# Gated cross-attention with a mixture of experts: where the routing's small sums, factors and statistics are computed

## The chip, the cores and the metric

The kernel runs on one core of a Trainium2 chip. The core has five engines with instruction lists of their own: PE multiplies matrices, DVE does vector work, ACT applies functions, POOL does small vector work and issues indirect DMAs (gathers and scatters), and SP issues plain DMAs. Each engine takes its list in order; an instruction that waits holds up all behind it on that engine. The metric is device time in microseconds for one execution, the median of the runs. Less is better.

## The reference, cut to what matters

There are four batches of 512 tokens with 256 features. First comes cross-attention in which a token looks at four neighbouring rows of a context, then a feed-forward layer with eight experts, of which each token uses two:

```python
x = x + tanh(g_xattn[0]) * xattn(layernorm(x), ctx_1024, itok, Wq, Wkv, Wo)   # rows itok, itok-1, itok-2, itok-3
h = layernorm(x)
probs = softmax(h @ gate_w.T)                 # 8 experts
top_v, top_i = top_k(probs, 2)
out = 0
for e in range(8):
    y = silu(h @ w1[e] + b1[e]) @ w2[e] + b2[e]     # 256 -> 1024 -> 256
    out += y * (weight of e if e is in top_i, else 0)
x = x + tanh(g_ffn[0]) * out
```

All is in float32.

## The kernel before, in words

The 2048 tokens are 16 tiles of 128, four to a batch. The kernel has two overlapping parts.

**Attention, a tile at a time.** `rows_of` gathers a tile's four context rows from a DRAM table of projected keys and values (POOL, L240; three buffers, two tiles ahead; the first gather needs the table of batch 0, stored at L228). `stage_ask` makes the queries (PE, `pq`, L426). `stage_attend` multiplies and sums (DVE, `prod`, `sc`, L439 to L485; the exponential `ex` on ACT, L459) and leaves `ao` (or `v`, for the first tiles). `stage_out` turns it (`pa`, L497/L499), copies it (`aoT`, ACT L512), multiplies by the output weights (`po`, L515), and DVE adds the residual (`x_sb`, L518), the gate's logits (`lg`, L526) and the statistics of the second norm (L257, L258). The first norm's statistics, which give `rsa`, the factor inside `ex`, are made for a whole batch by `normalise_first`: four pairs of BATCH_NORM instructions on DVE and two instructions on POOL (L266, L268).

**Routing.** Tiles form groups of 2, 2, 1, 1, 1, 1, 2, 2, 2, 2. When a group's last tile is out, `stage_route` finds the two best experts per token (`best`, `which`), the exponentials of the logits (`exg`, L592), their sum `gs`, the one-hot choices `pick`, and `pos`, the row of the scratch table `xs` to which each token's copy goes. Each expert owns a region of `xs`. `pos` needs a running count of tokens per expert: `run` (DVE, L565) over earlier tiles, multiplied by a matrix of ones on PE (L571), plus a triangular product within the tile (L568), plus the region's first row `ebase` (L595). POOL computes `rs`, the norm's factor (L266, L268), ACT writes the normalised `rows` (L609), and POOL scatters them (L377), two scatters per tile. In order not to hold up tile 4, the code lets its `rs` go ahead of half of the scatters of the group before it (L582).

`queue` runs after groups from tile 4 on (after tiles 5, 6, 7, 8, 10, 12, 14 and 16, counted as tiles finished). From the counts (`pn`, L666) it names the next full blocks of 128 rows, each with an expert and a first row: 3, 2, 2, 2, 4, 4, 4, 4 of them, and all that is left at the end. At its end it updates `took`, `take`, `issued` and `nextrow` (L727 to L733).

**Blocks.** There are 37 blocks in this run's main path. SP loads a block's weights (`w1s`, L752) and its rows (`xg`, L770, which waits for the scatters so far). PE turns the rows (`pxg`, L783), DVE copies them (`xgT`, L786), PE multiplies up (`ph`, L798), ACT applies Silu (`hT`, L810), PE multiplies down (`py`, L825), DVE weighs (`yw`, L836), and POOL adds the result to the output (L839).

What orders the work: `in_order` chains DVE's attention and routing instructions in the order in which they are written. The order on the other engines, and where the blocks' instructions come between, is fixed when the program is built. So PE's list mixes pieces of attention with pieces of blocks, and the mix can't adapt at run time.

On SP, the first loads are `xT_sb` and `x_sb` of batch 0 (L137, L140), then the store of the first table (L228), then `x_sb` of batch 1 (L322).

Of the kernel before, what the change touches and what calls it, by code (L numbers as in the profile page):

```python
# [9 lines left out]
F32 = mybir.dt.float32  # L10
# [6 lines left out]
P = 128  # L17
# [6 lines left out]
def gated_xattn_moe(  # L24
# [117 lines left out]
    first_loads = [load_xT(0), load_x(0)]  # L142
# [142 lines left out]
    with tc.tile_pool(  # L285
        name="ps_t", bufs=1, space=bass.MemoryType.PSUM
    ) as ps_t:
        with in_order(PE, mybir.EngineType.DVE):
# [7 lines left out]
            stored = project_near(kv_first, ps_t, src0, 0)  # L296
# [25 lines left out]
    behind(load_x(1), stored)  # L322
# [29 lines left out]
    def _layers(ctx, is_near):  # L352
# [16 lines left out]
        run = keep.tile([P, NT + 1, E], F32, name="run")  # L369
        nc.vector.memset(run[:, 0, :], 0.0)  # L370
# [159 lines left out]
        def stage_route(g):  # L530
# [15 lines left out]
            for j in range(GT):  # L546
# [4 lines left out]
            nc.vector.tensor_tensor(  # L551
                ex, lg, best[:, :, 0:1].to_broadcast([P, GT, E]), ALU.subtract
            )
# [9 lines left out]
            for j in range(GT):  # L563
                t = t0 + j
                nc.vector.tensor_add(run[:, t + 1, :], run[:, t, :], pick[:, j, :])  # L565
# [5 lines left out]
            nc.tensor.matmul(  # L571
                pp,
                all_one,
                run[:, tiles, :].rearrange("p t e -> p (t e)"),
                start=False,
                stop=True,
            )
# [12 lines left out]
            behind(named, root)  # L590
            for j in range(GT):
                nc.scalar.activation(ex[:, j, :], ex[:, j, :], AF.Exp, scale=rs[:, j : j + 1])  # L592
            yield
            place = gate.tile([P, GMAX, E], F32, tag="place", name=f"place_{g}")[:, 0:GT]
            nc.vector.tensor_tensor(  # L595
                place,
                pp.rearrange("p (t e) -> p t e", e=E),
                ebase.unsqueeze(1).to_broadcast([P, GT, E]),
                ALU.add,
            )  # L600
            nc.vector.tensor_tensor(
                hot, hot, place.unsqueeze(2).to_broadcast([P, GT, TOPK, E]), ALU.mult
# [4 lines left out]
            nc.vector.scalar_tensor_tensor(nm, mv[:, :, 0], -1.0, rs, ALU.mult, ALU.mult)  # L607
# [10 lines left out]
            gs = gate.tile([P, GMAX], F32, tag="gs", name=f"gs_{g}")[:, 0:GT]  # L618
            nc.vector.tensor_reduce(gs, ex, AX.X, ALU.add)
            nc.vector.reciprocal(gs, gs)  # L620
            yield
# [19 lines left out]
        issued = keep.tile([P, E], F32, name="issued")  # L641
        nc.gpsimd.memset(issued, 0.0)
# [14 lines left out]
        took = keep.tile([P, E + 1], F32, name="took")  # L657
        nc.gpsimd.memset(took, 0.0)

        def queue(tiles, w, last=False):  # L660


            q = len(ready)
# [367 lines left out]
```

## Time and profile before

| | us |
|---|---|
| median of 3 runs | 399.97 (399.18 to 400.34) |
| the profiled execution | 399.22 |
| its span, first to last instruction | 397.5 |
| PE busy | 343.4 |
| DVE busy | 195.7 |
| ACT busy | 160.1 |
| POOL busy | 131.3 |
| first product of the first block (`ph`, L798) | starts at 85.2 |

A float32 product is two records of PE (MATMUL) and two weight loads (PEld) in the profile: what is called a pair below. In lines of the timeline the columns are the start and the busy time in us, the engine, the line, the operation, the tiles written and read, the shapes, the number of instructions merged and, in brackets, how long the engine had been idle and what released it.

### The profile page before, as it was taken

Reading aid. Unit: us, or ns where it says so; the run is one execution under the profiler, and the core shown is the slowest. Engines: PE = TensorE matmul, PEld = TensorE weight load, DVE = VectorE, ACT = ScalarE, POOL = GpSimd, SP = SyncE. Lnnn points to the kernel's source line nnn. Section 1 sums busy time; section 2 is a strip of 40 time slices with the busy share of each in tenths; the row PEclk is TensorE's granted clock in tenths of the full one; section 3 lists DMA queues with packets and bytes.
Section 4 is the critical chain, followed back from the end, with each engine's and each line's share of the span. In section 5 each row is a group of like instructions: output and inputs, shape, how many; then the busy total and the mean of one; then the engine's idle time right before and its main releaser. Section 6 shows DMA issues by size and latency. Waiting matters only on the chain. (4 is left out here: it accounts for less than half of the span.)

```text
span 397.5 us, 7304 instructions
## 1 busy us (share of the span) xinstructions
PE 343.4 (86%) x2153; PEld 306.9 (77%) x2153; DVE 195.7 (49%) x663; ACT 160.1 (40%) x445; POOL 131.3 (33%) x164
## 2 busy tenths in 40 slices
PE   4877646089999989999999999999999999999960
PEld 1545534078998989898889989999999999999950
DVE  2288797879789989798947301101111111111000
ACT  1121202027756666767576334234243342342410
POOL 4421444513365354453724322112112122121311
PEclk9869696579999999999999999999999999999995
DMA  7899999589969988987667897776767767755111
GB/s 259 269 399 423 419 425 378 177 287 313 299 187 343 237 274 280 336 238 233 205 158 189 281 222 234 236 196 164 246 176 211 214 171 235 195 167 143 18 28 17
DMA packets 43577, 94.22 MB, mean 237 GB/s; under 512 B 14844, under 2 KB 31996, under 8 KB 35720
## 3 DMA queue, kind: packets, MB, share of 16 engines
q1 hardware_dynamic: 33506, 66.23, 51.2%
q0 software_dynamic: 9168, 26.09, 23.0%
q10 hardware_dynamic: 854, 1.33, 1.0%
q8 instruction: 21, 0.34, 0.3%
q14 instruction: 28, 0.23, 0.2%
HBM read 79.90 MB, written 13.73 MB: 236 GB/s over the span
## 5 line engine op out<-in xcount | busy, mean ns | idle before, releaser
L798 PE MATMUL ph<-xgT,w1s 128*128 128x128 f32 x1184 | 143.0, 276 | 0.0
L798 PEld LDWEIGHTS ph<-xgT,w1s 128*128 128x128 f32 x1184 | 140.3, 192 | 2.3
L825 PE MATMUL py<-w_sb,hT 128*128 x592 | 135.7, 380 | 1.4 <-DVE yw L836 0.7
L810 ACT ACTIVATE hT<-ph,b1s 128x128 f32<-128x128 f32 x296 | 83.6, 372 | 113.6 <-issue 95.7
L825 PEld LDWEIGHTS py<-w_sb,hT 128*128 128x128 f32 x592 | 109.2, 190 | 15.7 <-issue 2.1
L839 POOL DMA_INDIRECT out<-yw,ms x37 | 58.7, 1586 | 158.3 <-issue 69.5
L836 DVE SCALAR_TENSOR_TENSOR yw<-py,ms,b2s 128x256 f32<-128x256 f32 x37 | 17.8, 482 | 76.3 <-PE py L825 72.4
L786 DVE COPY xgT<-pxg 128x256 f32<-128x256 f32 x37 | 15.6, 421 | 69.5 <-PE pxg L783 69.4
L377 POOL DMA_INDIRECT xs<-rows,pos x32 | 35.0, 1094 | 30.6 <-ACT rows L609 7.3
L240 POOL DMA_INDIRECT g<-near,idx_near x16 | 17.6, 1098 | 37.4 <-DVE v L472 23.3
L439 DVE TENSOR_TENSOR prod<-pq,g 128x1024 f32<-128x1024 f32 x16 | 19.4, 1213 | 5.9 <-DMA g<-near,idx_near 5.9
L426 PE MATMUL pq<-wqg_sb,xT_sb 128*128 128x264 f32 x64 | 20.5, 449 | 1.5 <-DVE prod L439 1.1
L515 PE MATMUL po<-wo_sb,aoT 128*128 128x264 f32 x64 | 19.8, 436 | 2.0 <-ACT aoT L512 1.4
L472 DVE TENSOR_TENSOR v<-g,pr 128x1024 f32<-128x1024 f32 x16 | 19.6, 1224 | 0.5
L810 ACT ACT_TABLE_LOAD x13 | 16.7, 1283 | 7.7 <-issue 5.2
L442 DVE TENSOR_REDUCE sc<-prod 128x64 f32<-128x1024 f32 x16 | 19.5, 1217 | 0.4
L868 ACT ACTIVATE b2s<-b2s,ms 128x256 f32<-128x256 f32 x37 | 19.5, 532 | 0.0
L426 PEld LDWEIGHTS pq<-wqg_sb,xT_sb 128*128 128x128 f32 x64 | 14.0, 225 | 5.2 <-DVE prod L439 2.2
L497 PE MATMUL pa<-ident,ao 128*128 128x128 f32 x24 | 5.6, 308 | 13.2 <-DVE ao L485 13.1
L515 PEld LDWEIGHTS po<-wo_sb,aoT 128*128 128x128 f32 x64 | 12.1, 207 | 5.6 <-ACT aoT L512 4.0
L783 PE MATMUL pxg<-ident,xg 128*128 128x128 f32 x74 | 14.5, 278 | 1.5 <-DMA xg<-xs 1.5
L497 PEld LDWEIGHTS pa<-ident,ao 128*128 128x128 f32 x24 | 3.3, 165 | 14.5 <-issue 11.6
(128 smaller groups left out, 262.6 us busy)
## 6 DMA issues: line engine op xcount, KB each, us to landing
w1s<-in_w SPq DMA_DIRECT2D x37, 1024.0 KB, 5.4
w_sb<-in_w SPq DMA_DIRECT2D x8, 1024.0 KB
b2s<-in_b SPq DMA_DIRECT2D x37, 128.0 KB, 5.2
xg<-xs SPq DMA_DIRECT2D x37, 128.0 KB, 5.5
xT_sb<-in_xT SPq DMA_DIRECT2D x4, 512.0 KB, 11.3
x_sb<-in_x SPq DMA_DIRECT2D x4, 512.0 KB
out<-x_sb SPq DMA_DIRECT2D x6, 256.0 KB
xs<-padrow SPq DMA_DIRECT2D x9, 136.0 KB, 3.7
```

Source lines behind the costliest of these rows:

```text
L377: i = nc.gpsimd.indirect_dma_start(out=xs, out_offset=bass.IndirectOffsetOnAxis(ap=where, axis=0), in_=rows, in_offset=None,).ins
L426: nc.tensor.matmul(pq, xT_sb[:, t, k, :], wqg_sb[:, k, :], start=(k == 0), stop=(k == KD - 1))
L439: seen[t] = nc.vector.tensor_tensor(prod, pq[:, 0:D].unsqueeze(1).to_broadcast([P, KW, D]), gt[:, :, 0:D], ALU.mult).ins
L442: nc.vector.tensor_reduce(sc.rearrange("p o h -> p (o h)"), prod.rearrange("p o (h d) -> p (o h) d", d=HD), AX.X, ALU.add,)
L472: nc.vector.tensor_tensor(v.rearrange("p o (h d) -> p o h d", d=HD), gt[:, :, D : 2 * D].rearrange("p o (h d) -> p o h d", d=HD), pr.unsqu ...
L515: nc.tensor.matmul(po, aoT[:, k, :], wo_sb[:, k, :], start=(k == 0), stop=(k == KD - 1))
L798: m = nc.tensor.matmul(ph[:, i, :], w1s[:, k, ts(f, P)], xgT[:, k, :], start=(k == 0), stop=(k == KD - 1),).ins
L810: hidden = nc.scalar.activation(hT[:, f, :], ph[:, i, :], AF.Silu, bias=b1s[:, f : f + 1]).ins
L825: m = nc.tensor.matmul(py, hT[:, f, :], w2_sb[:, bass.ds(be_v * NF + f, 1), :].rearrange("p o d -> p (o d)"), start=(f == 0), stop=(f == N ...
L836: outs[s] = nc.vector.scalar_tensor_tensor(yw, py, ms[:, 0:1], b2s, ALU.mult, ALU.add).ins
L839: acc = nc.gpsimd.indirect_dma_start(out=out, out_offset=bass.IndirectOffsetOnAxis(ap=ms[:, 1:2].bitcast(I32), axis=0), in_=yw, in_offset= ...
L868: behind(nc.scalar.activation(b2s, b2s, AF.Copy, scale=ms[:, 0:1]).ins, hidden)
```

## The change

There are five edits.

1. `x_sb` of batch 1 is loaded right after that of batch 0, before the store of the first table, and `normalise_first(1)` is called right after `normalise_first(0)`, ahead of the first tile's attention, not after it.
2. `run` starts from the regions' first rows (in one partition only, since the ones-matrix sums over partitions), so the addition of `ebase` (`place`, L595) goes. `run` has one entry for a group, not for a tile, and its additions move from DVE to POOL. The product of ones with `run` now takes the count before the group; within a group the second tile adds a product with the first one's `pick`, and `queue` adds one product for each tile of the group.
3. ACT's exponential takes the logits themselves, with `-best * rs` as its bias, and gives the sum `gs` through its accumulator output. The subtraction (L551) and the sum (L619) go from DVE. The factors `less` (`-rs`, `-best * rs`) and `nm` are computed on POOL, three instructions for a group.
4. `issued` is gone: `queue` subtracts `nextrow`. `took`, `take` and `nextrow` are computed on POOL.
5. The reciprocal of `gs` is taken after `pos` as before, but now waits for ACT directly.

```diff
-    first_loads = [load_xT(0), load_x(0)]
+    first_loads = [load_xT(0), load_x(0), load_x(1)]
...
-    behind(load_x(1), stored)
...
-        run = keep.tile([P, NT + 1, E], F32, name="run")
-        nc.vector.memset(run[:, 0, :], 0.0)
+        run = keep.tile([P, len(GROUPS) + 1, E], F32, name="run")
+        nc.gpsimd.memset(run[:, 0, :], 0.0)
+        nc.gpsimd.tensor_copy(run[0:1, 0, :], ebase[0:1])
+        picks = {}
...
-            nc.vector.tensor_tensor(
-                ex, lg, best[:, :, 0:1].to_broadcast([P, GT, E]), ALU.subtract
-            )
+            gs = gate.tile([P, GMAX], F32, tag="gs", name=f"gs_{g}")[:, 0:GT]
...
-            for j in range(GT):
-                t = t0 + j
-                nc.vector.tensor_add(run[:, t + 1, :], run[:, t, :], pick[:, j, :])
+            picks[g] = pick
...
-            nc.tensor.matmul(
-                pp,
-                all_one,
-                run[:, tiles, :].rearrange("p t e -> p (t e)"),
-                start=False,
-                stop=True,
-            )
+            for j in range(GT):
+                for k in range(j):
+                    nc.tensor.matmul(
+                        pp[:, j * E : (j + 1) * E], all_one, pick[:, k, :], start=False, stop=False
+                    )
+                nc.tensor.matmul(
+                    pp[:, j * E : (j + 1) * E],
+                    all_one,
+                    run[:, g, :],
+                    start=False,
+                    stop=(j == GT - 1),
+                )
...
+            less = stat.tile([P, 3, GMAX], F32, tag="less", name=f"less_{g}")[:, :, 0:GT]
+            nc.gpsimd.tensor_scalar(less[:, 0], rs, -1.0, None, ALU.mult)
+            nc.gpsimd.tensor_tensor(nm, mv[:, :, 0], less[:, 0], ALU.mult)
+            nc.gpsimd.tensor_tensor(less[:, 1], best[:, :, 0], less[:, 0], ALU.mult)
             for j in range(GT):
-                nc.scalar.activation(ex[:, j, :], ex[:, j, :], AF.Exp, scale=rs[:, j : j + 1])
+                nc.scalar.activation(
+                    ex[:, j, :],
+                    lg[:, j, :],
+                    AF.Exp,
+                    bias=less[:, 1, j : j + 1],
+                    scale=rs[:, j : j + 1],
+                    accum_out=gs[:, j : j + 1],
+                )
+            count = run[:, g, :]
+            for j in range(GT):
+                nc.gpsimd.tensor_add(run[:, g + 1, :], count, pick[:, j, :])
+                count = run[:, g + 1, :]
             yield
-            place = gate.tile([P, GMAX, E], F32, tag="place", name=f"place_{g}")[:, 0:GT]
...
-            nc.vector.scalar_tensor_tensor(nm, mv[:, :, 0], -1.0, rs, ALU.mult, ALU.mult)
...
-            nc.vector.tensor_reduce(gs, ex, AX.X, ALU.add)
+            yield
             nc.vector.reciprocal(gs, gs)
-            yield
...
-            nc.tensor.matmul(pn, all_one, run[:, tiles, :], start=True, stop=True)
+            GT = GROUPS[g][1]
+            nc.tensor.matmul(pn, all_one, run[:, g, :], start=True, stop=False)
+            for j in range(GT):
+                nc.tensor.matmul(pn, all_one, picks[g][:, j, :], start=False, stop=(j == GT - 1))
...
-                nc.vector.tensor_scalar(took[:, 1 : E + 1], ends, float(w), None, ALU.min)
+                nc.gpsimd.tensor_scalar(
+                    took[:, 1 : E + 1], ends, float(w), float(P), ALU.min, ALU.mult
+                )
                 take = gate.tile([P, E], F32, tag="take", name=f"take_{q}")
-                nc.vector.tensor_tensor(take, took[:, 1 : E + 1], took[:, 0:E], ALU.subtract)
-                nc.vector.scalar_tensor_tensor(
-                    issued, take, float(P), issued, ALU.mult, ALU.add
-                )
-                nc.vector.scalar_tensor_tensor(
-                    nextrow, take, float(P), nextrow, ALU.mult, ALU.add
-                )
+                nc.gpsimd.tensor_tensor(take, took[:, 1 : E + 1], took[:, 0:E], ALU.subtract)
+                nc.gpsimd.tensor_add(nextrow, nextrow, take)
...
             normalise_first(0, after=gathers)
+            normalise_first(1, after=gathers)
...
-                if i in (0, RAMP, RAMP + 2):
+                if i in (RAMP, RAMP + 2):
                     normalise_first(1 + (i + 1) // TPB)
```

## The prediction

> **What bounds the kernel now.** I read the page's 40 slices first, then busy time by stretches, then the chain of waits, then the timeline of the stretches where PE is not full. The chain that ended last says nothing here (four pieces at the very end), so the bound is read from the stretches. In the first fence (busy time by stretches; columns: length, busy time and count of PE, PEld, DVE, ACT, POOL, then granted clock, DMA share, GB/s), see that PE does next to nothing from 70 to 80 us while DVE is full, and is full without a break after 240.
>
> ```profile
> 70.00:80.00 10.00, 0.20 (x1) 0.23 (x2) 8.80 (x35) 0.57 (x2) 5.57 (x7) 0.57 0.53 175
> ...
> 100.00:110.00 10.00, 10.00 (x74) 9.54 (x75) 8.07 (x38) 6.92 (x18) 3.70 (x4) 1.00 0.96 298
> ...
> 240.00:280.00 40.00, 40.00 (x272) 37.55 (x271) 4.86 (x11) 14.26 (x48) 7.73 (x5) 1.00 0.73 210
> ```
>
> From 85 us to about 385 us PE is never idle for long: all its waits from 84 to 240 us add up to about 4 us, most of it for `ao`. So the time is (when the first block's `ph` starts, 85 us) + (PE's work behind it) + (about 4 us). The change can act on the first by shortening DVE's path up to 80 us, and on the second by the products that it adds. The next fence, the timeline around the first group of one tile (tile 4), shows the path to the first block: POOL computes `rs`, then issues the last two scatters of the group before, and only then copies `tokid` (L586) and scatters tile 4; DVE meanwhile goes on (L620).
>
> ```profile
> 67.80 0.62 POOL L268 TENSOR_TENSOR rs<-v_b,mhalf 128x1 f32<-128x1 f32 x1
> ...
> 68.61 1.06 POOL L377 DMA_INDIRECT xs<-rows,pos  x1 [0.20 <-issue]
> ...
> 69.69 0.16 DVE L620 RECIPROCAL gs<-gs 128x1 f32<-128x1 f32 x1
> ...
> 69.98 0.96 POOL L377 DMA_INDIRECT xs<-rows,pos  x1 [0.30 <-issue]
> ...
> 70.95 0.20 POOL L586 COPY rows<-tokid 128x8 int32<-128x8 int32 x1
> ```
>
> The third fence, a little later, shows what a small product costs once PE is full: `pp`, `pp`, `pn` and the next `ph` start 0.22 us apart, though only 8 columns move.
>
> ```profile
> 86.45 0.36 PE L568 MATMUL pp<-pick,upto 128*128 128x8 f32 x2
> ...
> 86.67 0.37 PE L571 MATMUL pp<-run,all_one 128*128 128x8 f32 x2
> ...
> 86.89 0.37 PE L666 MATMUL pn<-run,all_one 128*128 128x8 f32 x2
> ...
> 87.11 2.70 PE L798 MATMUL ph<-xgT,w1s 128*128 128x128 f32 x22
> ```
>
> The fourth, for the out stage of tile 0: `po`, then `pq`, then DVE's residual.
>
> ```profile
> 31.49 1.16 PE L515 MATMUL po<-wo_sb,aoT 128*128 128x264 f32 x4 [0.46 <-ACT aoT L512]
> ...
> 32.49 1.05 PE L426 MATMUL pq<-wqg_sb,xT_sb 128*128 128x264 f32 x4
> ...
> 33.70 0.48 DVE L518 SCALAR_TENSOR_TENSOR x_sb<-po,tg,x_sb 128x256 f32<-128x256 f32 x1
> ```
>
> **The change, part by part** (later is plus).
>
> *1. Statistics of batch 2 first.* Their eight DVE instructions stand at 25.75 to 27.88, 2.13 us on DVE's path. They move to 14.1, where DVE waits 5.89 us for the first gather: 2.13 us saved there. But on SP the load of `x_sb` (512 KB) now stands ahead of the table's store, for which the first gather (13.50) waits. Behind it wait the second and third gather on POOL and `prod` on DVE. Bounds for the delay d: none, if the load only fills the idle share of the DMA engines (0.72 to 0.83 busy from 10 to 13 us); 1.9 us, if 0.52 MB go ahead at the 272 GB/s of 11 to 12 us. I take 0.5: both loads and the store had passed by 14 us anyway (share 0.25 from 14 to 15). On POOL the two-instruction chain for batch 2 is split around the third gather; its first half needs the statistics, about 16.3 us, and that gather started at 16.47, so nothing is lost.
>
> What is late next: the built order puts `pq` of tile 3 ahead of `po` of tile 0. `pa` of tile 0 ends at 31.04 (+d; it hangs on `ex` of tile 0, not on the moved statistics), then `pq` about 1.0, then `po` 1.16: L518 starts at 33.25+d, not 33.70. DVE would be ready at 31.57+d, and waits 1.7 us. So of 2.13 us saved only 0.45 survive, less d: **+0.05** (-0.45 to +1.45). The deleted memset (0.07 us, in a wait for a load) counts nothing; POOL's added copy of `ebase` delays only the second gather by 0.2, which is read only at 27.88.
>
> *2. Groups of tiles 0-1 and 2-3.* DVE loses subtraction, two `run` additions, `place`, `nm` and the sum, but its list then waits for `gs`. In the built order POOL adds the first `pick` to `run` **before** `rs`. So in the first group `rs` starts after `pick`, about 42.85 instead of 42.08. Then on POOL come `tokid`, an addition, and three small instructions, priced by L266 and L586 at 0.19 each and 0.15 to 0.27 apart: ends about 44.45. ACT does one `rows` (0.55) and then both exponentials (0.49 for two): the reciprocal starts about 45.5, not 45.24. Meanwhile `pp` has grown from four records to eight, at 0.24 each at the slow clock of that stretch (0.66 mean), and lands at about 44.6 against 44.34: no cover is left for an early finish either. With something for the accumulator and the bias operand, which no row shows (0 to 0.3): +0.35. Second group, same sum: 64.1 instead of 63.54, and on ACT `aoT` of tile 3 now stands behind both `rows` and both exponentials (63.09 becomes 64.6), so `po` (2.13 at the slow clock) ends near 67.1 and L518 (66.28) is +0.85. Together **+1.2** (0.5 to 2).
>
> [...]
>
> *3. Group of tile 4.* The built order on POOL reads: two scatters, first half of `rs`, `rs`, two scatters, `tokid`, `less`, the `run` addition, `nm`, `less` again, two scatters. The code moves only `rs` ahead of the older scatters, so the new factors stand behind them. DVE's reciprocal waits for ACT's exponential, that for `less`, and that for the scatters. By the rows: `rs` ends 68.42, `tokid` starts 2.53 later (70.95), then about 1.0 for the small ones, 0.3 for the exponential (L592), 0.05 to 0.1 per handover: reciprocal 3.75 after `rs`, where it was 1.27 (69.69). **+2.5** (2.0 to 3.0). Queued behind the waiting reciprocal are `left` and all of the first `queue`, hence the first `w1s` load, and the attention of tile 5. `rows` of tile 4 and its two scatters shift by nearly as much, hence `xg`.
>
> *4. Tail of the first `queue`.* L727 to L733, 0.58 us of DVE, go to POOL, which has time there: **-0.5**. `nextrow` is next read one tile later.
>
> So the first `ph` starts about **3.2 us later** (2 to 6), since both `pa` of tile 4 (waiting for DVE) and `xg` shift by about as much.
>
> *5. Products on the full PE.* After the first block each of the four groups of two gets two more pairs (8), the queues after tiles 6, 7, 8 one each (3), those after 10, 12, 14, 16 and the last one two each (10): 21 pairs at 0.22 = **+4.6** (3.2 at 0.15, the closest spacing of two such records; 6.1 at the 0.29 that two weight loads took at the slower clock near 80 us, L497). Nothing hides them: PE has no gap there.
>
> *6. DVE from 85 to 205 us.* It loses some 0.8 us per group and 0.6 per queue, and waits for the exponentials instead. PE's 4 us of waits can shrink: -1.5 (-4 to 0). Against that, in the last two groups the built order on ACT puts the eight Silus of a block between the two tiles' exponentials, with table loads on both sides (2.18 + 2 x 1.28 us by L810's rows): DVE's reciprocal, and the `xgT` copy behind it, wait nearly 5 us, against 3.6 us that PE spends in `py`: +1.0 (0 to 4). Together **-0.5**.
>
> [...]
>
> **Sum:** 0.05 + 1.2 + 2.5 - 0.5 + 4.6 - 0.5 = +7.3. Against the profiled execution (399.22, span 397.5 and 1.7 around it): 406.5. That execution stands 0.75 below the median of 399.97, inside the spread of the runs (399.18 to 400.34), so I leave the forecast at **406.5**.
>
> **Rivals.**
> - *The start gets earlier (faster).* If tile 4's factors did not wait for scatters and `pq` did not delay `po`, then 2.1 (statistics) + 0.5 (queue tail) + 0.8 for each of three groups = 5.0 us earlier, and with PE's 4 us of waits gone: 4.6 - 5.0 - 3 = -3.4, or 396. It decides where the first `ph` starts before about 82 us. For it: DVE is over 90% busy before 80 us. Against: the order of POOL's list is fixed. 0.09.
> - *The start holds (402.5).* Waits and savings cancel before 85 us, since `xg`'s landing (6.6 us after the last scatter) has slack; only the products are paid, less 2 of PE's waits. 0.20.
> - *The split exponentials stall PE (411).* Two stalls of 2 us or more, where `xgT` comes after `py` has ended. 0.15.
> - *Nothing measurable (400).* 0.04.
>
> **How the numbers follow.** The forecast's case (404 to 409) has 0.52. Leaving out the faster case and part of the tail above, the range is 401 to 410.5. About 0.3% is what a measurement of this kernel can tell from no change: faster 0.09, same 0.04, slower 0.87.
>
> **What would show it.** After: the reciprocal of tile 4's group about 3.5 us behind its `rs`, with DVE idle for ACT; L518 of tile 0 waiting for `po`; the first `ph` at 87 to 90 us; from then on 21 more pairs and PE still full. It is wrong if the first `ph` comes before 85, or if PE's added pairs fall into waits that are gone.

## The result and the profile after

The changed kernel takes 411.27 us (408.94 to 412.25), the kernel before beside it 400.15 us: a ratio of 1.030 (95% interval 1.0249 to 1.035). It is slower by about 11 us, where the forecast was 406.5 with 410.5 as its upper end. The profiled execution took 412.14 us, with a span of 410.4.

Five times say where the span's 12.9 us went, for the one profiled execution of each kernel. They come from PE's timeline and from stretches of 2 us each (idle: length less PE's busy time; half clock: length times one less the granted clock).

| | before | after | difference |
|---|---|---|---|
| first full run of `ph` starts | 85.24 | 90.51 | +5.3 |
| PE idle behind it, up to 360 us | 4.6 | 6.8 | +2.2 |
| time lost to a lower clock behind it | 0.0 | 4.2 | +4.2 |
| the rest of PE's time up to the last block's `py` (377.18, 391.88) | 287.3 | 290.4 | +3.0 |
| from there to the end | 20.3 | 18.5 | -1.8 |

The last row belongs to POOL: it issues the last scatter 1.7 us after its `yw` is done before, and 0.3 us after it in the changed kernel. Why is not shown.

The stretches of the changed kernel show both losses that are not work. The columns are those of the stretches before. The last line is the kernel before, for the stretch that differs most.

```profile
70.00:80.00 10.00, 2.35 (x11) 1.43 (x10) 5.52 (x32) 1.15 (x4) 6.64 (x15) 0.67 0.34 100
80.00:90.00 10.00, 4.15 (x11) 3.13 (x12) 7.98 (x20) 1.07 (x3) 2.74 (x4) 0.50 0.75 265
...
230.00:240.00 10.00, 6.53 (x35) 6.56 (x36) 3.30 (x15) 1.21 (x5) 3.19 (x2) 0.66 0.79 221
240.00:280.00 40.00, 40.00 (x272) 37.52 (x271) 5.08 (x12) 14.89 (x50) 7.72 (x5) 1.00 0.76 206
```

```profile
230.00:240.00 10.00, 9.22 (x63) 8.15 (x62) 1.33 (x3) 3.74 (x14) 1.99 (x2) 1.00 0.95 264
```

From 70 to 80 us DVE is busy for 5.52 us where it was 8.80: it waits. From 230 to 240 PE is busy for only 6.53 us (9.22 before), and at a clock of 0.66 (1.00 before). From 240 to 280 PE is full in both.

**The start.** The timeline around tile 4's group:

```profile
71.06 0.61 POOL L268 TENSOR_TENSOR rs<-v_b,mhalf 128x1 f32<-128x1 f32 x1
...
71.87 1.06 POOL L379 DMA_INDIRECT xs<-rows,pos  x1 [0.20 <-issue]
...
73.23 0.96 POOL L379 DMA_INDIRECT xs<-rows,pos  x1 [0.30 <-issue]
74.20 0.20 POOL L590 COPY rows<-tokid 128x8 int32<-128x8 int32 x1
74.36 0.27 POOL L596 TENSOR_SCALAR less<-rs 128x1 f32<-128x1 f32 x1
...
74.73 0.20 POOL L597 TENSOR_TENSOR nm<-mv,less 128x1 f32<-128x1 f32 x1
74.88 0.20 POOL L598 TENSOR_TENSOR less<-best,less 128x1 f32<-128x1 f32 x1
75.11 0.39 ACT L600 ACTIVATE exg<-lg,less,rs 128x8 f32<-128x8 f32 x1 [3.65 <-POOL less L598]
75.41 0.19 ACT L600 ACTIVATION_READ_ACCUMULATOR exg<-lg,less,rs 128x1 f32 x1
...
75.63 0.16 DVE L633 RECIPROCAL gs<-gs 128x1 f32<-128x1 f32 x1 [2.99 <-ACT exg L600]
```

`rs` ends at 71.67; two older scatters come before the factors `less`, and the reciprocal of `gs` follows 3.96 us after `rs` (1.27 before). ACT waits 3.65 us for POOL, DVE 2.99 us for ACT. `left`, whose `pn` is done at 72.67, stands behind that reciprocal in DVE's list and starts at 75.97. The sum that the exponential's accumulator takes is read by an instruction of its own, 0.19 us.

PE feels this through the next tile's `ao` (tile 5), which DVE makes behind all of this, and whose turning (`pa`) stands ahead of the first block in PE's list. The first line is the kernel before, the second the changed one:

```profile
79.80 0.66 PE L497 MATMUL pa<-ident,ao 128*128 128x128 f32 x2 [10.67 <-DVE ao L485]
```

```profile
85.02 0.66 PE L499 MATMUL pa<-ident,ao 128*128 128x128 f32 x2 [12.36 <-DVE ao L487]
```

**The out stage of tile 0**, the place of the first step:

```profile
32.11 1.06 PE L428 MATMUL pq<-wqg_sb,xT_sb 128*128 128x264 f32 x4
...
33.01 1.05 PE L517 MATMUL po<-wo_sb,aoT 128*128 128x264 f32 x4
34.95 0.48 DVE L520 SCALAR_TENSOR_TENSOR x_sb<-po,tg,x_sb 128x256 f32<-128x256 f32 x1
```

As in the built order, `pq` goes first; the residual starts at 34.95 (33.70 before).

**The small products**, in PE's timeline of the last group:

```profile
213.68 0.37 PE L567 MATMUL pp<-pick,upto 128*128 128x16 f32 x2
213.90 0.37 PE L575 MATMUL pp<-run,all_one 128*128 128x8 f32 x2
214.12 0.37 PE L572 MATMUL pp<-pick,all_one 128*128 128x8 f32 x2
214.35 0.37 PE L575 MATMUL pp<-run,all_one 128*128 128x8 f32 x2
214.57 0.37 PE L677 MATMUL pn<-run,all_one 128*128 128x8 f32 x2
```

A pair each 0.22 us, as forecast. From one record's start to the next one's, all `pp` and `pn` behind the first `ph` take 9.29 us where they took 4.43: +4.9.

**The end of the routing**, timeline from 216 us, which the prediction did not foresee:

```profile
216.14 0.39 ACT L600 ACTIVATE exg<-lg,less,rs 128x8 f32<-128x8 f32 x1
...
222.12 0.39 ACT L600 ACTIVATE exg<-lg,less,rs 128x8 f32<-128x8 f32 x1
...
223.00 0.16 DVE L687 TENSOR_TENSOR left<-pn,nextrow 128x8 f32<-128x8 f32 x1
...
223.88 1.01 POOL L379 DMA_INDIRECT xs<-rows,pos  x1 [6.35 <-DVE upb L698]
...
226.14 0.38 PE L791 MATMUL pxg<-ident,xg 128*128 128x128 f32 x2
...
227.74 0.96 POOL L379 DMA_INDIRECT xs<-rows,pos  x1 [0.30 <-issue]
...
228.77 0.28 POOL L738 TENSOR_SCALAR took<-ends 128x8 f32<-128x8 f32 x1
...
229.41 0.20 POOL L743 TENSOR_TENSOR nextrow<-nextrow,take 128x8 f32<-128x8 f32 x1
229.64 0.17 DVE L687 TENSOR_TENSOR left<-pn,nextrow 128x8 f32<-128x8 f32 x1 [3.79 <-POOL nextrow L743]
...
232.95 0.42 DVE L794 COPY xgT<-pxg 128x256 f32<-128x256 f32 x1
...
233.47 6.43 PE L806 MATMUL ph<-xgT,w1s 128*128 128x128 f32 x32 [3.50 <-issue]
```

Two queues follow each other here: the one after tile 16 (`left` at 223.00) and the last one, whose `left` needs the `nextrow` of the first at once. `nextrow` is now on POOL, behind four scatters, one every 1.27 to 1.31 us (the lines show the first and the last). So `left` waits 3.79 us, the whole last queue shifts, and DVE copies `xgT` only at 232.95, though its `pxg` was done at 226.5. PE idles 3.50 us, and then needs 6.43 us for 32 records that take 3.73 just before (at 222.57): its granted clock is 0.50 from 232.1 to 239.0. The two exponentials of the last group stand 6.0 us apart, with eight Silus between, and the four scatters come behind the second. In the kernel before, the second `left` waits for nothing:

```profile
217.69 0.15 DVE L676 TENSOR_TENSOR left<-pn,issued 128x8 f32<-128x8 f32 x1
```

### The profile page after: what moved, and what is told of

Same layout as the page of the kernel before. It is cut to its first block, busy times and chain, and to the rows that moved or that the text cites. A ratio compares the mean times of both kernels' runs of the same rounds, so it can differ in the third digit from the quotient of the medians.

```text
span 410.4 us, 7409 instructions
## 1 busy us (share of the span) xinstructions
PE 353.9 (86%) x2205; PEld 316.2 (77%) x2205; DVE 185.2 (45%) x573; ACT 165.0 (40%) x463; POOL 147.4 (36%) x235
## 5 line engine op out<-in xcount | busy, mean ns | idle before, releaser
L806 PEld LDWEIGHTS ph<-xgT,w1s 128*128 128x128 f32 x1184 | 142.1, 196 | 5.9 <-issue 3.9
L847 POOL DMA_INDIRECT out<-yw,ms x37 | 59.7, 1613 | 146.4 <-DVE yw L844 125.5
L428 PE MATMUL pq<-wqg_sb,xT_sb 128*128 128x264 f32 x64 | 21.9, 477 | 3.0 <-DVE prod L441 2.6
L517 PE MATMUL po<-wo_sb,aoT 128*128 128x264 f32 x64 | 20.7, 452 | 3.6 <-ACT aoT L514 3.6
L623 ACT ACTIVATE rows<-x_sb,nm,rs 128x256 f32<-128x256 f32 x16 | 9.3, 594 | 15.0 <-POOL nm L597 15.0
```

The lines of the kernel that those rows point to most:

```text
L428: nc.tensor.matmul(pq, xT_sb[:, t, k, :], wqg_sb[:, k, :], start=(k == 0), stop=(k == KD - 1))
L517: nc.tensor.matmul(po, aoT[:, k, :], wo_sb[:, k, :], start=(k == 0), stop=(k == KD - 1))
L806: m = nc.tensor.matmul(ph[:, i, :], w1s[:, k, ts(f, P)], xgT[:, k, :], start=(k == 0), stop=(k == KD - 1),).ins
L847: acc = nc.gpsimd.indirect_dma_start(out=out, out_offset=bass.IndirectOffsetOnAxis(ap=ms[:, 1:2].bitcast(I32), axis=0), in_=yw, in_offset= ...
```

## Experiments

Each ratio is against the kernel before on the same chip, with its 95% interval. The changed kernel stands at 1.030.

**One part undone: the early statistics.**

```diff
-    first_loads = [load_xT(0), load_x(0), load_x(1)]
+    first_loads = [load_xT(0), load_x(0)]
+    behind(load_x(1), stored)
-            normalise_first(1, after=gathers)
-                if i in (RAMP, RAMP + 2):
+                if i in (0, RAMP, RAMP + 2):
```

> The changed kernel with its first edit alone undone: batch 2's inputs are loaded behind the near store again, and its statistics stand behind tile 0's. Theory (the load ahead of the table's store delays the first gather by 2.2 us, 13.50 to 15.71, and of the statistics' 2.13 us only part is saved, L518 of tile 0 going from 33.70 to 34.95): first gather back near 13.5, first ph 1.25 earlier, time -1.2 us against the changed kernel (about 410). Rival (moving the statistics saves their 2.13 us of DVE's path, and the later start has its cause in the gate): +2 us (about 413).

Measured: 411.47 us, 1.0328 (1.0291 to 1.0365). The first gather is back at 13.94 and tile 0's residual starts at 34.10 (0.85 earlier), but the first `ph` moves by 0.6 only (89.92), and the gap at 230 is still 3.49. Both theories missed. A shift of 0.6 in single traces says little: two traces of one kernel below (the lean one) have the first `ph` at 83.59 and 85.06.

**One part undone: took, take and nextrow on DVE.**

```diff
-                nc.gpsimd.tensor_scalar(took[:, 1 : E + 1], ends, float(w), float(P), ...)
+                nc.vector.tensor_scalar(took[:, 1 : E + 1], ends, float(w), float(P), ...)
```

and the same for `take` and `nextrow`.

> The changed kernel with took, take and nextrow back on VectorE; the exponentials are not touched, so those of the last group stay split by eight Silus and two table loads. Theory (the last queue's left, 229.64, waits 3.79 us for nextrow, which stands on GpSimd behind four scatters; TensorE then idles 3.5 us at 230 and loses some 2.7 us more at a lower clock): the idle time at 230 goes, the clock of 230 to 240 is near 1, time -5 to -6 us (about 405.5), less 0.2 us per queue where VectorE bounds the start. Rival (the split exponentials hold VectorE, whose reciprocal waits 2.90 us for them, and with it xgT): a gap of 2 us or more stays, time 0 to -1 us.

Measured: 411.4 us, 1.0298 (1.0252 to 1.0345). The gap at 230 is gone, and with it both half-clock periods there, as the theory said; but the time is as long as that of the changed kernel. In this trace (414.95 us, the longest of its four executions) a half-clock period starts at 218.9 (1.7 us lost), right behind the group's small products, and PE waits 1.6 us for `xg` at 243 with another such period behind it. That `xg` waits for the last scatters; the last one is issued at 230.17 (227.74 in the changed kernel), behind the late exponentials.

**One part undone: tile 4's factors ahead of the older scatters.**

```diff
-            if t0 == RAMP - 1:
-                for i in scatters[-TOPK * GROUPS[g - 1][1] // 2 :]:
-                    behind(i, root)
...
+            if t0 == RAMP - 1:
+                for i in scatters[-TOPK * GROUPS[g - 1][1] // 2 :]:
+                    behind(i, last_less)
```

> The changed kernel with the two older scatters put behind tile 4's three small factor instructions on GpSimd, where the changed kernel has them ahead. Theory (tile 4's reciprocal comes 3.96 us after rs instead of 1.27 because of these scatters, and VectorE's queue behind it starts the first block): reciprocal within 2 us of rs, first ph 2 to 2.7 us earlier, time -2 to -2.7 us (about 409). Rival (the first block waits for xg, whose last scatter moves by as much as the factors gain): first ph within 0.5 us of the changed kernel's, time within 0.5 us.

Measured: 411.13 us, 1.0281 (1.0233 to 1.033). The first `ph` starts at 88.14, 2.4 earlier, as the theory said; 0.8 of this stands already at tile 4's residual (68.72, not 69.53), ahead of the edit. The gain is given back: at the end of the routing `ph` starts again at 232.31, behind a gap of 3.42, with 5.1 us of half clock in all.

**One part undone: the products.** `run` per tile again, additions on DVE, one product for a group and one for a queue:

```diff
-            for j in range(GT):
-                for k in range(j):
-                    nc.tensor.matmul(pp[:, j * E : (j + 1) * E], all_one, pick[:, k, :], ...)
-                nc.tensor.matmul(pp[:, j * E : (j + 1) * E], all_one, run[:, g, :], ...)
+            nc.tensor.matmul(pp, all_one, run[:, tiles, :].rearrange("p t e -> p (t e)"), ...)
```

> The changed kernel with one running count per tile again (the additions on VectorE) and the products of before: one per group and one per queue, 21 pairs fewer behind the first block and some fewer ahead of it. Theory (a pair costs 0.22 us on a full TensorE, nothing hides it): -4.6 us behind the first block, and 0 to -1 in the groups ahead of it, so about 406. Rival (TensorE waits longer elsewhere, so that the pairs only fill its waits): within 1 us of the changed kernel.

Measured: 410.82 us, 1.0283 (1.0246 to 1.0321). `pp` and `pn` take 4.20 us again, 5.1 less, but the gap before 231.35 has grown from 3.5 to 6.0 us. The rival was right on the time, and for its reason.

**The products alone, on the kernel before.**

```diff
-            nc.tensor.matmul(pn, all_one, run[:, tiles, :], start=True, stop=True)
+            nc.tensor.matmul(pn, all_one, run[:, g, :], start=True, stop=False)
+            for j in range(GT):
+                nc.tensor.matmul(pn, all_one, picks[g][:, j, :], start=False, stop=(j == GT - 1))
```

and the same for `pp`, with `run` per group on DVE.

> The kernel before with only the change's products: one running count per group, the products for its earlier tiles added in TensorE. Theory (0.22 us for each added pair on a full TensorE, 21 of them): +4 to +5 us against the kernel before (about 404.5). Rival (they fall into waits, or their spacing is that of before's nearest pairs at 0.15): +0 to +3 us.

Measured: 400.12 us against 398.73, 1.0037 (1.0005 to 1.0069): +1.5 us of the 4.7 that the records take (9.17 less 4.43). PE's idle time falls from 4.6 to 2.3. Single executions reach from 398.63 to 405.31 us; the trace (401.87) has two half-clock periods, at 143.0 and 218.1, both behind a burst of small products, with no wait of PE over 0.4 us in the 10 us ahead of either.

**The early statistics alone, on the kernel before.**

```diff
-    first_loads = [load_xT(0), load_x(0)]
+    first_loads = [load_xT(0), load_x(0), load_x(1)]
...
+            normalise_first(1, after=gathers)
```

> The kernel before with only the first edit: batch 2's inputs loaded ahead of the near store, its statistics ahead of tile 1's. Theory (first gather 2.2 us later, residual of tile 0 1.25 us later, the rest of the start shifts with it): first ph +0.5 to +1.3, time +1 us (about 401). Rival (the 2.13 us of statistics leave VectorE's path): -1 to -2 us.

Measured: 399.25 against 398.73, 1.0014 (0.9999 to 1.0029); first `ph` at 86.67. No gain; the loss is 0.6 us, with an interval from none to 1.2.

**Three parts undone together** (the three diffs for products, `took` and tile 4's factors).

> The changed kernel with three things undone together: products as before, took, take and nextrow on VectorE, tile 4's factors ahead of the older scatters. Left of the change: the early statistics, the exponentials with bias and accumulator, the factors on GpSimd, the regions' first rows in the running count. Theory (the three are worth 4.6, 5 to 6 and 2 to 2.7 us, and add up): 398 to 400. Rival (what is left still holds the start 3 us later, and the three overlap): 402 to 404.

Measured: 406.06 us, 1.02 (1.0161 to 1.0238). The first `ph` is back at 85.0, there is no half-clock period and no gap over 1.8 us, yet some 8 us stay (6.4 to 9.5). PE idles 9.3 us in many pieces; DVE waits 11.2 us for `exg` in seven waits, where the kernel before waits 2.1. Both theories missed. The waits point at the gate (edits 3 and 5: the exponentials, their factors on POOL and the reciprocal behind them), which the next runs take by itself.

**The leaner bookkeeping alone, on the kernel before** (of edits 2 and 4 what leaves the engines as they are).

```diff
+        nc.gpsimd.tensor_copy(run[0:1, 0, :], ebase[0:1])
-            nc.vector.tensor_tensor(place, pp..., ebase..., ALU.add)
-            nc.vector.tensor_tensor(left, pn, issued, ALU.subtract)
+            nc.vector.tensor_tensor(left, pn, nextrow, ALU.subtract)
-                nc.vector.scalar_tensor_tensor(issued, take, float(P), issued, ALU.mult, ALU.add)
-                nc.vector.scalar_tensor_tensor(nextrow, take, float(P), nextrow, ALU.mult, ALU.add)
+                nc.vector.tensor_add(nextrow, nextrow, take)
```

> The kernel before with only the change's leaner bookkeeping: the running count starts with the regions' first rows (no place, no pad_f), issued is gone, nextrow is one addition on VectorE. Theory (two VectorE instructions of about 0.2 us fewer in each group and two in each queue, on the path to the first block): first ph 0.4 to 1.2 us earlier, time -0.4 to -1.2 us against the kernel before. Rival (the three groups' ends are set by other engines): within 0.3%.

Measured: 395.25 against 398.73, 0.9921 (0.989 to 0.9953): faster than both kernels, and by more than expected (3.2 us, interval 1.9 to 4.4). In its trace the first `ph` is at 83.59 and PE idles 3.4 us, where the kernel before has 85.24 and 4.6.

**The gate undone.**

```diff
+            nc.vector.tensor_tensor(ex, lg, best[:, :, 0:1]..., ALU.subtract)
-            nc.gpsimd.tensor_scalar(less[:, 0], rs, -1.0, None, ALU.mult)
-            nc.gpsimd.tensor_tensor(nm, mv[:, :, 0], less[:, 0], ALU.mult)
-            nc.gpsimd.tensor_tensor(less[:, 1], best[:, :, 0], less[:, 0], ALU.mult)
-                nc.scalar.activation(ex[:, j, :], lg[:, j, :], AF.Exp, bias=..., scale=..., accum_out=...)
+                nc.scalar.activation(ex[:, j, :], ex[:, j, :], AF.Exp, scale=rs[:, j : j + 1])
+            nc.vector.scalar_tensor_tensor(nm, mv[:, :, 0], -1.0, rs, ALU.mult, ALU.mult)
+            nc.vector.tensor_reduce(gs, ex, AX.X, ALU.add)
```

The reciprocal goes back to its old place with it.

> The changed kernel with the gate's exponentials as before: VectorE subtracts the maximum, sums and makes nm; no less on GpSimd, no bias, no accumulator. Early statistics, products, counts, took and nextrow stay as in the changed kernel. Theory (single undoings of the other parts gave nothing; what is left is that VectorE waits for exponentials that stand behind three small instructions on GpSimd: 6.3 us in four waits after the first block, and 2.7 us in tile 4's group): first ph at 86 to 88 instead of 90.5, VectorE's waits for the exponentials near 2 us, time -4 to -6 us against the changed kernel (about 406). Rival (products and the nextrow wait on GpSimd hold the end whatever the gate does): first ph earlier, but the first ph after the last queue still near 232, time 0 to -1.5 us.

Measured: 403.28 us, 1.0093 (1.0055 to 1.0131), 8 us faster than the changed kernel, more than either theory had. Taking this one part out brings back most of the loss, though the change's products, statistics and POOL's `nextrow` are all still there. Its executions reach from 401.05 to 407.29 us, and the trace is of the longest. So the same kernel again:

> The changed kernel with the gate's exponentials as before, once more, for its trace. Theory (with whole exponentials the last queue's wait for nextrow is shorter than the changed kernel's 3.79 us, and TensorE's gap at 230 is gone with both half-clock periods): no gap of over 1 us between 215 and 240, no half-clock period, time 401 to 404. Rival (the gap stays, and the gain of 8 us came from the start): gap of 2 us or more, first ph at 85.

Measured: 400.63 and 406.28 us, 1.0107 (1.0034 to 1.0181); the trace is of the first. The first `ph` starts at 84.83, and the `pa` ahead of it, which waited for DVE in the changed kernel, is back at 79.42 (79.80 before, 85.02 in the changed kernel). In the trace of 407.29 us that `pa` is as early (79.92), but PE then waits for `xg`, and the first `ph` starts only at 89.38:

```profile
85.55 0.69 PE L785 MATMUL pxg<-ident,xg 128*128 128x128 f32 x2 [4.97 <-DMA xg<-xs]
```

So DVE's delay at the start goes with the gate; that load's late landing is another matter, and why it differs between two executions of one kernel is not shown. Timeline at the end of the routing in the trace of 400.63 us:

```profile
208.93 0.49 ACT L598 ACTIVATE exg<-exg,rs 128x8 f32<-128x8 f32 x2
...
215.22 0.20 POOL L737 TENSOR_TENSOR nextrow<-nextrow,take 128x8 f32<-128x8 f32 x1
215.45 0.17 DVE L681 TENSOR_TENSOR left<-pn,nextrow 128x8 f32<-128x8 f32 x1 [2.42 <-POOL nextrow L737]
...
216.95 3.79 PE L800 MATMUL ph<-xgT,w1s 128*128 128x128 f32 x32
```

Both exponentials run together. `left` still waits 2.42 us for `nextrow`, which this build puts behind two scatters, not four; PE has no gap over 1 us there and no half-clock period. So in the changed kernel the gap needs both: `nextrow` on POOL, and the gate's edit, with which the build puts four scatters ahead of it. Both theories were right in part: the gain is at the start and at the gap.

**The gate alone, on the kernel before**, and the same **with the factors ahead of the older scatters** (the diffs above, the other way round).

> The kernel before with only the change's gate: exponentials with bias and accumulator on ScalarE, the three small instructions for their factors on GpSimd, place, issued, products and counts as before. Theory (the gate is the largest part): first ph 2 to 4 us later than 85.2, VectorE's waits for the exponentials 8 us or more against 2.1, one group's exponentials split by eight Silus; time +4 to +7 us against the kernel before (about 404.5). Rival (alone, the gate's saved VectorE instructions pay for its waits): within 1.5 us.

> The kernel before with only the change's gate (405.51 us), but with tile 4's three factor instructions on GpSimd ahead of the two older scatters. Theory (the gate costs in two places: 2.5 us at the start, by the scatters ahead of tile 4's factors, and 3 us later, where VectorE's longer waits for the exponentials become waits of TensorE): first ph at 85 to 86 instead of 87.75, time -2 to -3 us against the gate alone (about 403). Rival (the start's gain is given back, as it was in the whole change): first ph earlier, time within 1 us of 405.5.

Measured: 405.51 us, 1.0171 (1.0124 to 1.0219), first `ph` at 87.75, DVE's waits for `exg` behind it 6.5 us; with the factors ahead 401.59 us, 1.0081 (1.0053 to 1.0109), first `ph` at 85.19. Timeline of the second around tile 4:

```profile
67.96 0.61 POOL L268 TENSOR_TENSOR rs<-v_b,mhalf 128x1 f32<-128x1 f32 x1
...
69.17 0.19 POOL L588 TENSOR_TENSOR less<-best,less 128x1 f32<-128x1 f32 x1
69.39 0.39 ACT L596 ACTIVATE exg<-lg,less,rs 128x8 f32<-128x8 f32 x1 [1.17 <-POOL less L588]
69.69 0.19 ACT L596 ACTIVATION_READ_ACCUMULATOR exg<-lg,less,rs 128x1 f32 x1
69.74 1.10 POOL L377 DMA_INDIRECT xs<-rows,pos  x1 [0.39 <-issue]
69.91 0.16 DVE L629 RECIPROCAL gs<-gs 128x1 f32<-128x1 f32 x1 [0.23 <-ACT exg L596]
```

The scatter now comes behind `less`, and the reciprocal 1.34 us after `rs`. So about half of the gate's cost is the scatters ahead of tile 4's factors (0.0090 of 0.0171, 3.6 us); some 3 us stay, and behind the first block PE idles 7.1 us instead of 4.6. The theory held, with a larger gain than it said (3.6 for 2 to 3).

**POOL's bookkeeping alone, on the lean kernel**, in all queues, and in all but the one ahead of the last.

```diff
-                nc.vector.tensor_scalar(took[:, 1 : E + 1], ends, ...)
+                eng = nc.vector if tiles == NT else nc.gpsimd
+                eng.tensor_scalar(took[:, 1 : E + 1], ends, ...)
```

(the second one; in the first all three are `nc.gpsimd`).

> The lean kernel (before with the regions' first rows in the running count, without place, pad_f and issued; 395.25 us) with took, take and nextrow moved to GpSimd. Theory (the last queue's left waits for nextrow, which stands behind four scatters on GpSimd): left waits 3 us or more, TensorE has a gap of 2 us or more near 215, and a half-clock period of 3.4 us or two behind it; time +3 to +6 us (about 399.5). Rival (the gap in the changed kernel comes from the split exponentials, which are whole here): within 0.5 us of the lean kernel, or 0.5 us faster for VectorE's lighter queues.

> The lean kernel with took, take and nextrow on GpSimd in every queue but the one ahead of the last, which computes them on VectorE. ScalarE's order is that of the lean kernel with all of them on GpSimd: the last group's two exponentials are split by eight Silus there too. Theory (the one queue ahead of the last makes the whole 7.6 us: left waits 3.7 us behind four scatters, TensorE idles 3.4 us at 218 and then runs two half-clock periods, 3.4 us more): gap and half-clock periods gone, time within 1 us of the lean kernel's 395.25. Rival (the split exponentials make the gap): gap of 2 us or more stays, 400 or more.

Measured: 402.86 us, 1.0078 (1.0047 to 1.0109), against 0.9921 for the lean kernel; and 398.97 us, 1.0023 (0.9996 to 1.005). The first one's timeline, then the second one's:

```profile
218.12 0.17 DVE L669 TENSOR_TENSOR left<-pn,nextrow 128x8 f32<-128x8 f32 x1 [3.72 <-POOL nextrow L725]
...
221.80 6.43 PE L788 MATMUL ph<-xgT,w1s 128*128 128x128 f32 x32 [3.41 <-issue]
```

```profile
215.19 0.17 DVE L669 TENSOR_TENSOR left<-pn,nextrow 128x8 f32<-128x8 f32 x1
...
218.93 3.81 PE L789 MATMUL ph<-xgT,w1s 128*128 128x128 f32 x32 [0.38 <-issue]
...
231.77 0.41 PE L774 MATMUL pxg<-ident,xg 128*128 128x128 f32 x2 [1.78 <-DMA xg<-xs]
```

In both, ACT has the last group's two exponentials 6.0 us apart, with eight Silus between. With `nextrow` on POOL in all queues there is the same picture as in the change: a wait of 3.72, a gap of 3.41, and two half-clock periods (6.43 us for 32 records). With the one queue on DVE all three are gone. So split exponentials alone do not make the gap: it takes `nextrow` on POOL in the queue ahead of the last; the rival is out. But only part of the loss comes back: 0.0055 of 0.0157 by the ratios, 3.1 of 6.6 us by the start of the last block's `py` (lean 373.6, then 380.2 and 377.1). What the theory left out shows in the trace: the last scatter is issued at 216.36, not 213.55 as in the lean kernel, and PE waits 1.78 us for `xg` at 230. The split exponentials would explain this, but no run parts them from POOL's bookkeeping in the other queues.

**Two parts undone together: products and took.**

> The changed kernel with two parts undone together, each of which gave nothing alone: took, take and nextrow on VectorE, and products and running counts as before. Theory (two limits stand side by side, TensorE's own work and the chain to the last queue; what one undoing gains, the other limit takes back): -4 to -6 us against the changed kernel (about 406), of which half from products, and no gap of TensorE near 230. Rival (the late start and the gate's waits hold all the rest): 0 to -1.5 us.

Measured: 411.94 us, 1.0284 (1.0218 to 1.0351). The theory of two limits side by side fell, and the time is that of the rival: the gap at 230 is gone and 4.8 us of small products too, yet PE idles 10.1 us (6.8 in the changed kernel), DVE waits 10.5 us for `exg`, and 3.4 us go to half clock.

**Ten more products in each group, of 8 columns and of 128.** On the kernel before, from tile 5's group on (seven groups, so 70 pairs; the expectation counts them from tile 4's and has 60 behind the first block), into a tile that nobody reads:

```diff
+            if t0 >= RAMP:
+                pd = ps_m.tile([P, P], F32, tag="m", name=f"pd_{g}")
+                for n in range(10):
+                    nc.tensor.matmul(pd[:, 0:E], all_one, pick[:, 0, :], start=(n == 0), stop=(n == 9))
```

(the second one writes all of `pd`, with the 8 columns repeated 16 times).

> The kernel before with ten more products of 8 columns in each of the groups from tile 4's on, into a tile that nobody reads. Theory (a burst of products with few columns counts as idle time for TensorE's clock, though TensorE never waits: 3.42 us at half clock, 1.71 us lost, behind many of the bursts): half-clock periods behind at least three of the six bursts after the first block, with no gap of TensorE of over 1 us ahead of them; time +13 us (60 pairs at 0.22) and 5 to 10 more. Rival (only gaps lower the clock): no such period, +13 us alone.

> The same ten added products in each group, but with 128 columns each (the same 8 columns, repeated). Theory (it is the few columns that lower the clock, and a pair of products costs 0.22 us with 8 columns or 128): no half-clock period behind the bursts, time near +13 us, 5 to 10 us less than with 8 columns. Rival (the columns do not matter for the clock): the same periods and the same time as with 8 columns, or more by the longer products.

Measured: 417.64 us, 1.0512 (1.0442 to 1.0582), and 415.11, 1.0428 (1.039 to 1.0466). Ten pairs take 2.38 us in the first and 2.48 in the second. The first one's timeline at a group, and two stretches from its table (columns as above); then the second one's:

```profile
146.38 2.38 PE L581 MATMUL pd<-pick,all_one 128*128 128x8 f32 x20
```

```profile
146.00:148.60 2.60, 2.60 (x25) 2.60 (x25) 1.56 (x9) 0.33 (x2) 0.94 (x1) 1.00 0.98 373
148.60:152.20 3.60, 3.60 (x19) 3.60 (x19) 2.25 (x14) 2.17 (x4) 0.70 (x1) 0.53 0.40 63
```

```profile
142.00:145.00 3.00, 3.00 (x29) 3.00 (x28) 1.22 (x8) 1.11 (x3) 0.41 (x1) 1.00 0.72 221
145.00:149.00 4.00, 4.00 (x36) 3.96 (x35) 3.54 (x20) 2.19 (x5) 3.08 (x4) 1.00 0.27 99
```

With 8 columns PE is busy all the time from 146.0 on, and still its clock is 0.53 from 148.6 to 152.2. Such periods follow the bursts at 85.2, 146.4 and 222.1, three of seven (the theory said three of the six behind the first; it was two): five periods, 8.5 us in all. With 128 columns there is none in the trace, and the mean clock of its four executions (0.939 to 0.953) lies above all four with 8 columns (0.914 to 0.931). So between these two kernels it is the few columns that lower the clock. The times differ by 2.5 us, not by 5 to 10, and the two intervals overlap: part comes back elsewhere, for PE idles 4.9 us in the wide one and 1.8 in the narrow one. The wide one's +16.7 us are nearly its 70 pairs alone (2.32 us from the first record of a burst to the next product, times seven: 16.2).

**The lean kernel once more.**

> The lean kernel (the kernel before with the regions' first rows in the running count, without place, pad_f and issued, nextrow as one addition on VectorE) once more, in five rounds. If its 0.9921 is a gain of its own: 0.990 to 0.995 of the kernel before, no half-clock period behind the first block. If it was a lucky order of runs: 0.997 or more.

Measured: 396.35 against 398.79 us, 0.9921 (0.989 to 0.9953), and no half-clock period that begins behind the first block's start. The gain stands. In this second trace the first `ph` is at 85.06, as before, and PE idles 2.9 us; so PE's shorter waits are in both traces, the earlier start in one. It is the version to keep.

## Why the prediction was wrong

The direction was right, the mechanism at the start too (+5.3 us there for a forecast of +3.2); the time lies 0.8 us above the range. By its own steps:

1. **Statistics first, +0.05: too small, and of little weight.** The delay d was taken as 0.5. In the two traces it is 2.2 us (gather at 15.71, not 13.50); over all traces the mean is 1.9 (15.8 in nine with the early load, 13.9 in eleven without), the upper bound itself. The residual of tile 0 came 1.25 later. But the kernel with the gate undone, which has the same early statistics, has the `pa` ahead of the first block as early as before, and the edit alone costs 0.0014 of the time.
2. **Groups of two tiles, +1.2: measured +2.0** (the residual of tile 4 is 3.25 late, 1.25 of it from step 1). The unknown was the exponential: 0.385 us each with the bias operand and the accumulator, for 0.295 with neither, and 0.19 more to read the accumulator. That is not all of it: with the gate alone this residual is at 66.85, 0.6 late, and with the gate undone at 66.36 and 67.25; the rest comes with gate and products together, and was not taken apart. (By the order of the residuals the `aoT` at 63.09 is tile 4's and the `pa` ahead of the first block is tile 5's, not tile 3's and 4's; no term of the sum changes by it.)
3. **Tile 4, +2.5: right in mechanism, and nearly in size**: the reciprocal comes +2.69 later behind `rs`. Taking the scatters out of the way moves the first `ph` by 2.4 in the changed kernel and by 2.6 with the gate alone; counted from tile 4's residual it is 1.6 and 2.1.
4. **The queue's tail, -0.5: the step that failed.** The saving came (0.6 us), but "nextrow is next read one tile later" does not hold for the queue after tile 16: the last queue follows at once. There the change pays 3.5 us of gap and 3.4 us of half clock, which the sum had at nothing. That `nextrow` on POOL is needed for it is shown by the pair on the lean kernel, where this one queue costs 2.2 us by the ratios and 3.1 by the traces, and by the changed kernel with `took` undone, whose gap is gone; that the gate's edit is needed too in the changed kernel, by the kernel with the gate undone.
5. **Products, +4.6: right as work, wrong as time.** The records take 4.9 us more. Alone they cost 1.5 us, and PE's waits shrink by 2.3 there: added pairs that fall into waits, which the prediction had named as a sign of being wrong. Undone, they only widen the gap.
6. **DVE from 85 to 205, -0.5.** Without the gap of 3.5, PE's idle time went from 4.6 to 3.3: close to the -1.5, but for another reason: the gate alone raises it from 4.6 to 7.2, and the products alone lower it to 2.3. The +1.0 for split exponentials was right to be there, wrong in form: they delay the last scatters and thus `xg`.

The rival of 411 us hit the number with half of its cause: `xgT` did come after `py` had ended, once and not twice, but the split exponentials alone leave a wait of 0.4 us there (0.38, in the kernel with that queue on DVE). None of the cases had PE's clock in it.

The parts don't add up when they are undone: products, `took`, statistics and tile 4's order give 1.1 us or less each, either way, which is inside their intervals; the gate gives 8. Added one at a time, they do: gate +0.0171, products +0.0037, statistics +0.0014, lean bookkeeping -0.0079, `took` on POOL +0.0157 of the time, together 0.0300, the measured ratio; with intervals of 0.0015 to 0.005 on each, so close a sum is partly luck. What stays open: why the kernel with products and `took` undone takes 4 to 6 us more than the gate alone, of which it differs only by things that cost little or help. The two builds put ACT's exponentials and PE's pieces in other places, and this was not taken apart.

## What to carry to other kernels

When a value moves to another engine, look for its earliest reader in every iteration, the last one above all, where two steps may follow each other without the work that lies between them elsewhere; and then for what stands ahead of the writer on its new engine. Undoing one part at a time says little when several late paths meet at one place: add the parts one at a time to the old kernel as well. The part that moves no work to another engine and only removes instructions was the one that paid.

## What the runs showed of the hardware

- **A half-clock period of PE lasted 3.4 us and cost 1.7 us**: one stands alone from 143.0 to 146.4 in the products' kernel, two follow each other from 232.1 to 239.0 in the changed one, at a granted clock of 0.50, behind a gap of 3.5 us.
- **No gap was needed.** In the kernel with ten added products, the clock fell behind 2.7 to 3.3 us of products with 8 or 16 columns, at three of seven such bursts; in the 10 us ahead of the two at 146.4 and 222.1 the longest wait of PE was 0.42 us. With 128 columns in the added ones, at nearly the same pace (2.48 us for ten pairs, not 2.38), it did not fall. What sets which of the bursts it follows is not shown.
- In the changed kernel the accumulator of each of ACT's gate exponentials is read by a second instruction of 0.19 us (16 of them, 3.0 us in all).
- In the changed kernel POOL takes 0.31 us for `took` (median of eight) and 0.20 for `nextrow`; `take` is 0.20 in four queues and 0.77 to 1.09 in the other four, and why is not shown. DVE takes 0.16, 0.17 and 0.17 for the three in the kernel with `took` undone. At the last queue the three take 0.68 us together, and the four scatters ahead of them some 5.
